# Rotary halves of queries and keys: exchanged by GpSimd's product with the sines in place of transfers

## Chip, cores and metric

The kernel runs on one core of a Trainium2 chip. The metric is the device time of one execution in microseconds (us). The parts of the core that appear below are PE (TensorE, the matmuls) and its weight loads (PEld), DVE (VectorE), ACT (ScalarE), POOL (GpSimd), SP (SyncE, here only a queue that issues transfers), and the 16 transfer engines. A transfer is issued by a queue (SP's, ACT's or POOL's own) and lands some microseconds later.

## What is computed

All data are float32. First comes an attention of one head of 256 over two batches of 1024 positions, with norms around it, and then a layer with 16 heads of 128 and a mixture of four experts. The change lies in the second layer's attention:

```python
q = (h @ wq + bq).reshape(b, s, H, HD).transpose(0, 2, 1, 3)
k = (h @ wk + bk).reshape(b, s, H, HD).transpose(0, 2, 1, 3)
...
def _rotate_half(x):
    x1, x2 = jnp.split(x, 2, axis=-1)
    return jnp.concatenate((-x2, x1), axis=-1)
...
q = q * cos + _rotate_half(q) * sin
k = k * cos + _rotate_half(k) * sin
scores = jnp.einsum('bhqd,bhkd->bhqk', q, k) / math.sqrt(HD)
scores = jnp.where(causal[None, None], scores, jnp.finfo(jnp.float32).min)
probs = jax.nn.softmax(scores.astype(jnp.float32), axis=-1).astype(q.dtype)
out = jnp.einsum('bhqk,bhkd->bhqd', probs, v)
```

Each of the 128 entries of a head's query or key is multiplied by a cosine, and the entry 64 places away is multiplied by a sine (negative for the first 64) and added.

## The kernel before

**Tiling.** A unit is one head of one batch: 8 rows of 128 queries against up to 1024 keys (the causal half). There are 32 units, two heads of the same weight columns form a pair, so 16 pairs. A query or key tile (`Twq`, `Twk`) has the 128 entries of a head along the 128 partitions and the 1024 positions along the free dimension. So the entry 64 places away lies in another partition, in the same column.

**Steps.** The order of the work is written out by hand: the whole kernel is a list of steps, one per row, and each step (`step`, L954) issues the scores of its row, then "fillers" that were put at this step, then work of earlier rows. One step in the steady part takes about 3.5 us. While PE goes through the 8 rows of a pair's first unit, the fillers compute the values of this pair and the keys of the next; in the second unit they compute the output product of the pair before and the queries of the next pair. Keys, queries and values of a pair are made by seven products in place of eight (`seven_products`, L539), which need sums of weight blocks that POOL computes (`weight_sums`, L522) and queries' weights scaled by POOL (`scale_queries`, L459).

**The rotation.** Whenever 512 columns of a query or key tile are written, by ACT (L502, L584) or DVE (L592), `rotated` (L465) is called. It issues two transfers on SP's queue at once: partitions 64 to 127 of the tile to partitions 0 to 63 of a tile `rot` (L469), and the other half (L470). `rot` has two buffers. It also appends `rest` to a list, and the step that follows, at its end, runs it: the tile times the cosines (L474), `rot` times the sines (L475), and their sum (L476), all 128 partitions by 512 columns, all on POOL. The argument `eng` of L474 is POOL's engine in every call, since `HELP` is empty. There are 128 rotations.

**The gathers.** The probabilities of a row are computed by DVE (L319, L321) and ACT (L326), scaled by ACT (L717) and transposed in blocks of 32 by DVE (L734) into one of two buffers (`pair_sb` for the first four rows of a unit, `x1`, shown as `x`, for the last four). Once four rows are there, `gather` (L745) issues 16 transfers on SP (L756), eight in each of two steps, that put the blocks into a tile `pT`. PE multiplies it with the values (L777). For the last four rows of a unit these products come 8 steps after the fourth row's scores, and 9 and 10 steps after them. So SP's queue, which issues strictly in its order, holds the exchanges of the rotation and the gathers, and the loads of the weights (L456) too.

**Other work on POOL.** The residual of the first layer (L436), the normalisation of `h` for the first batch (L204, in the last pair), and the issue of some loads. The cosines and sines are loaded once into `rope_sb` (L173).

Of the kernel before, what the change touches and what calls it, by code (L numbers as in the profile page):

```python
# [12 lines left out]
F32 = mybir.dt.float32  # L13
AF = mybir.ActivationFunctionType
ALU = mybir.AluOpType
# [3 lines left out]
P = 128  # L19
# [8 lines left out]
def kernel(  # L28
# [27 lines left out]
    nc = tc.nc  # L56
# [22 lines left out]
    bpool = ctx.enter_context(tc.tile_pool(name="bpool", bufs=2))  # L79
# [90 lines left out]
    bo_sb = const.tile([P, D], F32, name="bo_sb")  # L170
    nc.gpsimd.dma_start(bo_sb, bo.partition_broadcast(P))
    rope_sb = const.tile([P, 2, S], F32, name="rope_sb")
    nc.gpsimd.dma_start(rope_sb, rope.rearrange("k p s -> p k s"))  # L173

    par = const.tile([P, n_par], F32, name="par")

# [287 lines left out]

    def rotated(t, cs, eng=nc.gpsimd):  # L465

        rot = bpool.tile([P, 512], F32, tag="rot", name="rot")
        half = P // 2
        nc.sync.dma_start(rot[:half, :], t[half:, cs])  # L469
        nc.sync.dma_start(rot[half:, :], t[:half, cs])  # L470

        def rest():

            eng.tensor_tensor(t[:, cs], t[:, cs], rope_sb[:, 0, cs], ALU.mult)  # L474
            nc.gpsimd.tensor_tensor(rot, rot, rope_sb[:, 1, cs], ALU.mult)  # L475
            nc.gpsimd.tensor_tensor(t[:, cs], t[:, cs], rot, ALU.add)  # L476

        rope_later.append(rest)
# [9 lines left out]
    def b_project(u, name, n):  # L488

        g, b, hh = u  # L490
        bcol = cols["bq" if name == "wq" else "bk"] + g * GH + hh
        t = head_tile(u, name)
        pa = acc_tile()
        for c in range(DC):
            nc.tensor.matmul(
                pa,
                lhsT=wg[name][:, c, ts(hh, HD)],
                rhs=xT[:, c, ds(b * S + n * 512, 512)],
                start=(c == 0),
                stop=(c == DC - 1),  # L500
            )
        nc.scalar.activation(  # L502
            t[:, ts(n, 512)], pa, AF.Identity, bias=par[:, bcol : bcol + 1]
        )
        rotated(t, ts(n, 512))
# [33 lines left out]
    def seven_products(g, b, name, wide):  # L539
# [46 lines left out]
        def done(i, k):  # L586
            if not value:
                eng = nc.vector if (g, b) == pairs[1] and name in HELP else nc.gpsimd
                rotated(head_tile(heads[i - 1], name), ts(k - 1, 512), eng)
# [660 lines left out]
    s = A0 + (len(units) - 2) * NT  # L1250
# [154 lines left out]
```

## Time and profile before

| What | Value |
|---|---|
| time before, median of 3 runs | 1195.93 us (1195.11 to 1196.88) |
| the profiled execution, its own time | 1197.6 us |
| its span in the trace | 1195.8 us |
| instructions | 15503 |
| granted PE clock, mean | 0.996 |
| POOL's products of the rotation, L474 to L476 | 384, about 1.28 us each, 492.4 us |
| SP's issues: gathers / exchanges of halves | 976 / 256 |
| share of the 16 transfer engines taken by queue 1 | 51.4% |

The busy table gives each engine's busy time, its share of the span and the number of its instructions. A row of the groups of instructions has the line, engine, operation, output and inputs, the count, then busy time, mean duration of one in ns, and the idle time of the engine in front of them. Rows of transfer issues end with the median us from issue to landing. Rows of waits give who waited for whom, the total in us, the number of times and the longest one. A row of a queue in order of time gives its start, its length, engine, line and what it does, and in brackets the idle time before it. "x4" after a matmul counts records, of which a float32 matmul has two. A row of the table of stretches gives the stretch, its length, and the busy time of PE, PEld, DVE, ACT and POOL in it, then the PE clock, the share of the transfer engines, and GB/s. An engine that is named as the cause of a wait is inferred from semaphores, and can be another one that ended near by.

### The profile page before, as it was taken

To read this page: it belongs to the slowest core of one execution; us is meant where nothing else is said; L and a number is where in the kernel's file an instruction comes from. 1 tells how busy PE (TensorE), PEld (TensorE's weight loads), DVE (VectorE), ACT (ScalarE), POOL (GpSimd) and SP (SyncE) were. 2 spreads that over 40 slices of the span, in tenths; PEclk is the share of its full clock that TensorE was granted. 3 is DMA by queue.
4 is the path that set the end of the run, shared out by engine and by line. 5 is a ranking of instruction groups with operands and counts; after the bars stand their busy time and mean duration, and the time that the engine had idled before them with its cause. 6 is when DMAs were issued, how large, how long until landed. Compare 5 with 4: busy or idle time off the path is not lost.

```text
span 1195.8 us, 15503 instructions
## 1 busy us (share of the span) xinstructions
PE 1153.4 (96%) x4400; PEld 725.9 (61%) x4400; DVE 768.7 (64%) x1760; ACT 649.8 (54%) x1221; POOL 607.1 (51%) x594
## 2 busy tenths in 40 slices
PE   7999988989999999999999999999999999899997
PEld 5676644565656565656656565656565656556765
DVE  4554776656666766766676666666666567476565
ACT  3334356646565655656565656565656555453444
POOL 4005785566664747373837464666666667002100
PEclk9999999999999999999999999999999999999999
DMA  5001134777667667576666766666776767314011
GB/s 182 1 1 44 45 124 107 168 166 166 156 161 170 157 158 167 138 165 158 157 148 158 165 157 154 165 166 161 169 166 164 182 160 169 86 43 140 1 36 36
DMA packets 242391, 155.92 MB, mean 130 GB/s; under 512 B 21149, under 2 KB 223969, under 8 KB 241793
## 3 DMA queue, kind: packets, MB, share of 16 engines
q1 hardware_dynamic: 236720, 143.74, 51.4%
q0 software_dynamic: 2048, 5.94, 1.7%
q10 hardware_dynamic: 3536, 5.24, 1.2%
q8 instruction: 36, 0.59, 0.2%
q14 instruction: 51, 0.41, 0.1%
HBM read 20.62 MB, written 4.19 MB: 21 GB/s over the span
## 4 chain that ended last, share of the span: by engine, by line
PE 76%; SPq 7%; POOL 5%; DMA 5%; DVE 4%; issue 2%; ACT 1%; POOLq 0%; ACTq 0%; DVEq 0%
PE av L777 18%; PE sc L703 14%; PE pa L559 8%; PE pa L657 6%; SPq L756 6%; PE pa L550 5%; PE pa L1187 5%; PE pe L1210 4%; PE pc L559 3%; PE sc L360 3%; PE pa L382 2%; PE pc L550 2%; POOL rot L475 2%; DMA rot<-Twq 1%; POOL Twk L476 1%
## 5 line engine op out<-in xcount | busy, mean ns | idle before, releaser
L703 PE MATMUL sc<-Twk,Twq 128*128 128x512 f32 (+3 forms) x768 | 290.5, 487 | 2.2 <-ACT pr L326 1.3
L717 ACT ACTIVATE pr<-pr,rs 128x640 f32<-128x640 f32 (+1 forms) x244 | 190.0, 779 | 186.1 <-DVE rs L715 183.3
L777 PE MATMUL av<-pT,vg 128*128 128x512 f32 (+3 forms) x768 | 271.1, 491 | 19.2 <-DMA pT<-pair_sb 7.7
L326 ACT ACTIVATE pr<-sc,nmx 128x128 f32<-128x128 f32 (+7 forms) x272 | 201.0, 739 | 149.4 <-DVE nmx L321 122.8
L777 PEld LDWEIGHTS av<-pT,vg 128*128 128x128 f32 x768 | 142.4, 190 | 138.9 <-issue 101.5
L703 PEld LDWEIGHTS sc<-Twk,Twq 128*128 128x128 f32 x768 | 140.2, 191 | 125.3 <-issue 104.3
L321 DVE TENSOR_REDUCE nmx<-sc 128x1 f32<-128x128 f32 (+7 forms) x272 | 206.1, 758 | 9.4
L474 POOL TENSOR_TENSOR Twk<-Twk,rope_sb 128x512 f32<-128x512 f32 x64 | 82.0, 1280 | 201.2 <-DMA rot<-Twk 154.9
L319 DVE TENSOR_TENSOR sc<-sc,limit 128x128 f32<-128x128 f32 x272 | 79.6, 293 | 145.2 <-PE sc L703 129.8
L734 DVE STREAM_TRANSPOSE x<-pr 128x640 f32<-128x640 f32 (+1 forms) x124 | 128.8, 1039 | 60.8 <-DMA pT<-x 21.0
L475 POOL TENSOR_TENSOR rot<-rot,rope_sb 128x512 f32<-128x512 f32 x128 | 164.8, 1287 | 0.0
L657 PE MATMUL pa<-wo_g,aT 128*128 128x256 f32 x512 | 126.8, 381 | 0.0
L657 PEld LDWEIGHTS pa<-wo_g,aT 128*128 128x128 f32 x512 | 96.3, 191 | 35.2 <-issue 18.5
L474 POOL TENSOR_TENSOR Twq<-Twq,rope_sb 128x512 f32<-128x512 f32 x64 | 81.9, 1279 | 49.5 <-DMA rot<-Twq 33.1
L476 POOL TENSOR_TENSOR Twk<-Twk,rot 128x512 f32<-128x512 f32 x64 | 82.3, 1285 | 5.0
L476 POOL TENSOR_TENSOR Twq<-Twq,rot 128x512 f32<-128x512 f32 x64 | 81.4, 1271 | 5.0
L667 DVE TENSOR_TENSOR hx<-hx,pa 128x256 f32<-128x256 f32 (+1 forms) x124 | 52.4, 425 | 26.3 <-PE pa L657 24.0
L793 ACT ACTIVATE aT<-av,par 128x512 f32<-128x512 f32 x64 | 43.9, 686 | 42.8 <-PE av L777 42.7
L584 ACT ACTIVATE part<-pa,par 128x512 f32<-128x512 f32 x62 | 42.5, 687 | 39.7 <-PE pa L559 39.7
L734 DVE STREAM_TRANSPOSE pair_sb<-pr 128x128 f32<-128x128 f32 (+1 forms) x120 | 60.2, 502 | 2.8 <-DMA pT<-pair_sb 2.5
L1079 POOL TENSOR_TENSOR hx<-hx,x 128x256 f32<-128x256 f32 x16 | 12.7, 827 | 96.8 <-DVE hx L1219 84.6
L436 POOL TENSOR_TENSOR hx<-x,bo_sb 128x256 f32<-128x256 f32 x16 | 11.7, 733 | 90.7 <-ACT x L433 90.7
(193 smaller groups left out, 1620.7 us busy)
## 6 DMA issues: line engine op xcount, KB each, us to landing
pT<-x SPq DMA_DIRECT2D x496, 128.0 KB, 2.6
pT<-pair_sb SPq DMA_DIRECT2D x480, 64.0 KB, 2.1
rot<-Twk SPq DMA_DIRECT2D x128, 128.0 KB, 2.3
rot<-Twq SPq DMA_DIRECT2D x128, 128.0 KB, 2.3
wk_g<-in_L_ffn_wk_dram SPq DMA_DIRECT2D x9, 256.0 KB, 3.1
wq_g<-in_L_ffn_wq_dram SPq DMA_DIRECT2D x9, 256.0 KB, 3.2
wv_g<-in_L_ffn_wv_dram SPq DMA_DIRECT2D x9, 256.0 KB, 3.0
wo_g<-in_L_ffn_wo_dram SPq DMA_DIRECT2D x9, 256.0 KB, 3.0
```

The costliest lines, as they stand in the source:

```text
L321: nc.vector.tensor_reduce(nmx, sc[:, :L], AX.X, ALU.max, negate=True)
L326: nc.scalar.activation(pr[:, :L], sc[:, :L], AF.Exp, bias=nmx, accum_out=sm)
L474: eng.tensor_tensor(t[:, cs], t[:, cs], rope_sb[:, 0, cs], ALU.mult)
L475: nc.gpsimd.tensor_tensor(rot, rot, rope_sb[:, 1, cs], ALU.mult)
L476: nc.gpsimd.tensor_tensor(t[:, cs], t[:, cs], rot, ALU.add)
L550: nc.tensor.matmul(pa[:, ts(n, P)], lhsT=x[:, ts(n, P)], rhs=w, start=start and n == 0, stop=True, skip_group_check=True,)
L559: nc.tensor.matmul(pa, lhsT=w, rhs=x, start=start, stop=True, skip_group_check=True)
L657: nc.tensor.matmul(pa[:, ts(k, D)], lhsT=aT[g, b][:, hh, ts(i, P)], rhs=wg["wo"][:, hh, :], start=(hh == 0), stop=(hh == GH - 1),)
L703: nc.tensor.matmul(sc[:, ds(n0, n)], lhsT=qT[:, ts(i, P)], rhs=kT[:, ds(n0, n)], start=True, stop=True,)
L717: nc.scalar.activation(self.pr[:, :L], self.pr[:, :L], AF.Copy, scale=rs)
L734: nc.vector.transpose(z[:, i % 4, :n, :], self.pr[:, : n * 32].rearrange("p (m s) -> p m s", s=32))
L777: nc.tensor.matmul(cut(av), lhsT=vg[g, b][:, c, ts(hh, HD)], rhs=cut(pT[:, c, :]), start=(c == 0), stop=(c == i),)
```

## The change

`rotated` issues no transfers any more. Its deferred part takes the `rot` tile and lets POOL multiply partitions 64 to 127 of the tile by the sines, written to partitions 0 to 63 of `rot`, and then the other half the same way. The product with the cosines and the sum follow as before, on all 128 partitions. As the two inputs of such a product lie in the same partitions, the two halves of the sines are loaded exchanged, by two transfers in place of one for the whole table. On POOL, four instructions stand where three stood; the product with the cosines now comes after the ones with the sines, since it overwrites the tile that they read. On SP, the 256 exchanges are gone and nothing else is moved.

```diff
     rope_sb = const.tile([P, 2, S], F32, name="rope_sb")
-    nc.gpsimd.dma_start(rope_sb, rope.rearrange("k p s -> p k s"))
+    nc.gpsimd.dma_start(rope_sb[:, 0, :], rope[0])
+    for lo, hi in ((slice(0, P // 2), slice(P // 2, P)), (slice(P // 2, P), slice(0, P // 2))):
+        nc.gpsimd.dma_start(rope_sb[lo, 1, :], rope[1, hi])
...
     def rotated(t, cs, eng=nc.gpsimd):
 
-        rot = bpool.tile([P, 512], F32, tag="rot", name="rot")
-        half = P // 2
-        nc.sync.dma_start(rot[:half, :], t[half:, cs])
-        nc.sync.dma_start(rot[half:, :], t[:half, cs])
-
         def rest():
-
+            rot = bpool.tile([P, 512], F32, tag="rot", name="rot")
+            half = P // 2
+
+            for lo, hi in ((slice(0, half), slice(half, P)), (slice(half, P), slice(0, half))):
+                nc.gpsimd.tensor_tensor(rot[lo, :], t[hi, cs], rope_sb[hi, 1, cs], ALU.mult)
             eng.tensor_tensor(t[:, cs], t[:, cs], rope_sb[:, 0, cs], ALU.mult)
-            nc.gpsimd.tensor_tensor(rot, rot, rope_sb[:, 1, cs], ALU.mult)
             nc.gpsimd.tensor_tensor(t[:, cs], t[:, cs], rot, ALU.add)
 
         rope_later.append(rest)
```

## The prediction

> **What bounds the kernel now.** I read the busy table first, then the table of stretches, the waits of TensorE (PE), and last the queues in order of time around the longest wait.
>
> ```profile
> PE 1153.4 (96%) x4400; PEld 725.9 (61%) x4400; DVE 768.7 (64%) x1760; ACT 649.8 (54%) x1221; POOL 607.1 (51%) x594
> L475 POOL TENSOR_TENSOR rot<-rot,rope_sb 128x512 f32<-128x512 f32 x128 | 164.8, 1287 | 0.0
> rot<-Twk SPq DMA_DIRECT2D x128, 128.0 KB, 2.3
> rot<-Twq SPq DMA_DIRECT2D x128, 128.0 KB, 2.3
> 219.38:963.30 743.92, 734.99 (x2757) 450.64 (x2756) 486.38 (x1054) 443.05 (x833) 454.63 (x433) 1.00 0.69 162
> ```
>
> PE is busy for 96% of the span. The last line is the steady part, 26 units (one unit is one head of one batch): 734.99 of 743.92 us of PE, POOL (GpSimd) 454.63, clock 1.00. A unit takes 743.92/26 = 28.61 us, a pair of units 57.22. The quietest pair in the chain of waits (from the product at 609.09 to the one at 665.30) takes 56.21. So PE's own work is a floor: only what PE waits can be won, about 1.0 us a pair here, 13 us in all, and some at both ends.
>
> ```profile
> PE av L777 <- DMA pT<-pair_sb: 7.7, 3, 4.6
> PE av L777 <- DMA rot<-Twq: 6.7, 4, 3.6
> PE av L777 <- DMA pT<-x: 1.3, 1, 1.3
> ```
>
> These are PE's waits with their totals, counts and longest. All three are one kind: the product with the values (L777) waits for probabilities that L756's transfers bring. Eight of them, 15.7 us: 2.47 at 202.9, 3.58 at 249.0, 0.65 at 590.7, 0.69 at 817.8, 1.73 at 932.1, 1.34 at 990.6, 0.65 at 1003.7, 4.61 at 1020.7. Nothing else PE waits for is over 2.2 us between the loads at the start and the end. The SP queue ahead of the one at 249.0:
>
> ```profile
> 229.19 0.46 SPq L469 DMA_DIRECT2D rot<-Twq  x1
> 229.70 1.74 SPq L470 DMA_DIRECT2D rot<-Twq  x1
> 231.55 7.64 SPq L756 DMA_DIRECT2D pT<-x  x8
> 239.51 0.51 SPq L469 DMA_DIRECT2D rot<-Twq  x1
> 240.06 0.59 SPq L470 DMA_DIRECT2D rot<-Twq  x1
> 240.70 5.29 SPq L756 DMA_DIRECT2D pT<-x  x8
> ...
> 249.01 1.96 PE L777 MATMUL av<-pT,vg 128*128 128x512 f32 x3 [3.58 <-DMA rot<-Twq]
> ```
>
> SP issues without a gap, some 0.6 us a transfer, and the gathers stand in one line with the exchanges. The last gather is issued at 246.0, and lands 2.6 us later by the page's median: 248.6, just ahead of 249.0. A unit has 32 gathers (L756, 5.29/8 = 0.66 us each, 21.2 us) and 8 exchange issues (0.535 and 0.595 by their medians, 4.5 us): 25.7 of 28.6 us, before weight loads and waits. **SP's order of issue is the second bound behind PE.**
>
> **Part 1, the 256 exchanges leave SP.** This frees 4.5 us of issue a unit and the waits in which an exchange held the gathers: SP waited at L469 for POOL's addition (a free rot buffer) 19.8 + 8.9 us, for POOL's weight sums about 6.6, and early on for DVE's queries and keys 41.6. Twice 128 x 128 KB leave the transfer engines as well; I give that no price of its own.
> Per stall: at 249.0 four issues stood between 229.19 and 240.70, about 4 us with the 1.74, and the gathers in front of them were late by as much again; 3.58 goes. At 202.9 two issues (1.2 us) lie between the halves of the gather, and the one at 186.62 waited for DVE's sum in front of it: most of 2.47 goes. 590.7, 817.8 and 932.1 each have six or more issues within the last 14 us (over 3 us): 3.1 goes. 990.6, 1003.7, 1020.7: sixteen issues between 957.9 and 991.4, 9.1 us in a line with almost no gap till 1026; but weight loads on POOL's queue (issued 1011.7 to 1013.0) share the transfer engines, so I take 5.0 of 6.6. Sum 2.2 + 3.6 + 3.1 + 5.0 = 13.9.
> A product that starts after such a wait is recorded with 1.95 to 1.98 us for 1.72, and most pairs have one with a wait too short for the list. The 26 units hold 13 x 1.01 = 13.1 us above the quietest pair, 6.7 of it in the listed waits; of the other 6.4 I take half, 3.2. **Gain 17.1 us.**
> What is late next: the gather's own inputs, ACT's scaling (L717) and DVE's transposes (L734). Those waited for transfers themselves (26 us of DVE's L734 waits for gathers that still read its buffer), so they move forward with the gathers.
>
> **Part 2, POOL gets one product more per rotation.** Before, L474, L475, L476 start 1.23, 1.35 and 1.23 us apart: the third waits for POOL's own result and costs 0.12 more. 3.81 us. After: two products of 64 partitions, the product with the cosines (it overwrites what both read, so it waits), the sum (it waits). No row of the trace has a POOL product on 64 partitions, nor one that reads and writes different partitions.
> The nearest row is the 128 x 512 product: time there goes with the elements per partition (128x128 0.46, 128x256 0.73, 128x512 1.28 us), and a half has the same 512. So a half costs 1.23, and a rotation 1.23 + 1.35 + 1.35 + 1.23 = 5.16.
> The Trainium skill, "GPSIMD Engine Reference", section 2.1, says each of the eight cores serves its own 16 partitions and begins the next instruction once its share is done. If the core follows the written partition, the two halves use different cores and overlap: 3.9 us, almost no extra work. But the same page's split has a core reading and writing its own 16, and this product crosses over: that may cost extra, and the page has no price. I take the row, 5.16; ends 3.9 and 7.6 (each half twice the row).
> The page's section 4.1 speaks against the change: two-input elementwise work belongs on VectorE, GpSimd being about 2x slower. The rows agree on the ratio (POOL 1.28, DVE's L592 0.69), and by engine time the change loses: 128 x 1.35 = 173 us more on POOL. Read with the waits it doesn't: POOL idled 154.9 + 33.1 us before L474 for exchanges that are gone. By the rule +173 where POOL is the path, by the rows 0 where it isn't.
>
> ```profile
> POOL Twk L474 <- DMA rot<-Twk: 154.9, 28, 17.2
> POOL Twq L474 <- DMA rot<-Twq: 33.1, 18, 3.4
> 872.81 0.45 POOL L526 TENSOR_TENSOR S<-wv_g 128x128 f32<-128x128 f32 x1
> 876.63 0.38 PE L703 MATMUL sc<-Twk,Twq 128*128 128x128 f32 x2
> 880.78 1.05 PE L550 MATMUL pc<-S,lent 128*128 128x128 f32 x8
> ```
>
> The check is the fullest pair, where POOL also makes weight sums. Now its rotations start at 844.76, 850.72, 854.53, 859.50 (keys), 863.30, 869.01, eight sums from 872.81, then 876.62 and 880.43, done at 884.3. Afterwards, each free 2.4 us sooner: 842.4, 848.3, 853.5, 858.6, 863.8, 869.0, the first query done 869.0, the second 874.1, value sums done 876.0, key sums 877.9, end 888.2. PE reads the first query at 876.63 (7.6 us to spare), the value sums at 880.78 (4.8 to spare), the last queries a unit later. POOL's next work starts at 890. So it hides, with the 4.8 us as the cover: it is gone when twelve halves are 0.40 us dearer each, above 1.63.
> Other places: eight rotations from 101.7 to 138.1 end at about 146 instead; first readers are at 121.1 (keys and queries done 112) and 146.2 (done 123). Around 257.7 the query weights' load in POOL's queue goes 1.7 us later; its product is some 10 us off. The normalisation of h (L204, 1000.36 and 1006.90) stands behind the last rotation, which I put at 1001.3 for 999.7; PE transposes at 1009.7 and 1013.4, and comes some 2 us sooner relative to it: I charge 1.0.
>
> **Part 3, the sines** come as two loads and the cosines as one, in place of one: two more POOL issues of 0.74 us by 15 us, with POOL idle and the first rotation at 101.7. Nothing.
>
> **Sum.** Span 1195.8 - 17.1 + 1.0 = 1179.7; with 1.8 us around it the profiled execution would be 1181.5. That execution (1197.6) lies 1.7 above the median of the runs, 1195.93; median 1179.8, said as 1180.
>
> **Rivals.**
> A, likeliest: as above; 1173 to 1187, 0.66.
> B, the gathers are bound by their inputs, not by SP: freed issue time becomes SP idle time, and PE goes on waiting. For it: the eight gathers from 231.55 took 7.64 us, 2.4 more than 5.29, so some inputs were late. Against it: elsewhere SP runs gapless. A third to a half of the gain: 1187 to 1193, say 1190, 0.13.
> C, slower: the crossing makes each half dear. From 1.63 PE waits for value sums; from about 1.74 eight rotations and 7.1 us of sums and scaling no longer fit in 56.6 us, and POOL is the bound. At 2.46 a half a rotation takes 7.6, a pair 60.8 plus on average 4.9, 9.1 us too long; over some 14 pairs +127, less no gain: about 1320. For it: no row shows a crossing; against it: the flat dependence on elements. 0.14.
> D, it meets: halves near 1.6, gains and new stalls cancel; 1193.5 to 1198, 1196, 0.07. That the exchange goes on by transfers in another guise is excluded by the diff.
> If the halves overlap, A's time hardly moves, as POOL has cover already.
>
> A measurement of this kernel tells no change from one to about 0.2% (2.4 us). Faster: A and B, 0.79; same 0.07; slower 0.14. The range goes from A's low end, with 1 more for the unlisted waits, 1172, to 1195, which takes in B and part of D.
>
> **What would show it.** Right: no rot transfers on SP, gaps in SP's line between gathers, PE's waits at L777 under 5 us in all, POOL's halves at 1.23 to 1.28, POOL near 770 us busy, PE busy unchanged near 1153 to 1149. Wrong: halves at over 1.6 us, or PE waiting at L703 or L550 for POOL (C); L777 still waiting for pT with SP idle (B); a wait at the transposes of h near 1010 over 3 us.

## Result and profile after

| | before | after |
|---|---|---|
| median (4 runs each, beside one another) | 1195.52 us (1194.88 to 1196.88) | 1181.55 us (1179.69 to 1183.09) |
| ratio of the medians, 95% interval | | 0.9881 [0.9864, 0.9898] |
| the profiled execution | 1197.6 us, span 1195.8 | 1183.09 us, span 1181.3 |
| SP's exchanges of halves | 256 | 0 |
| queue 1, share of the transfer engines | 51.4% | 39.9% |

The change makes the kernel 1.2% faster; 1180.0 was predicted. The profiled execution is the slowest of the four after the change, so spans are compared with spans below.

The first view of the kernel after is the busy table with the groups of instructions and the queue's row (queue, packets, MB, share of the engines):

```profile
PE 1151.3 (97%) x4400; PEld 727.5 (62%) x4400; DVE 771.2 (65%) x1760; ACT 649.4 (55%) x1221; POOL 775.6 (66%) x724
L474 POOL TENSOR_TENSOR rot<-Twk,rope_sb 64x512 f32<-64x512 f32 x128 | 162.8, 1272 | 108.8 <-DVE Twk L592 102.2
q1 hardware_dynamic: 216240, 110.17, 39.9%
```

POOL has 168 us more to do and the kernel is faster. A product on 64 partitions takes 1.27 us, as one on 128 did (1.28). POOL now idles for the keys that DVE has yet to write, no longer for transfers.

Next, PE's waits in the kernel after (total, times, longest):

```profile
PE av L777 <- DMA pT<-pair_sb: 5.4, 2, 3.9
PE pt L340 <- DVE pr L719: 4.0, 2, 3.2
```

Of eight waits for gathers, 15.7 us, two are left, 5.4 us. The row of 3.2 us is new: before, that wait (at 149.73) was 1.44.

Last, the queue that changed. SP's largest wait between 280 and 900 us, after:

```profile
SPq L756 <- DVE rs L715: 131.0, 45, 5.1
```

and before:

```profile
SPq L469 <- POOL Twk L476: 12.3, 16, 1.1
```

SP waits 147.2 us in these 620 after, 31.1 before. Before, the gathers never waited long for the data they move: SP reached them late. After, SP stands at a gather until its blocks have been scaled and transposed (the cause named is DVE). The queue has turned from late to early.

**Where the time went.** The span is cut at the first score product of a unit; each stretch is the difference of two start times. The forecast's items are put into the stretch where their stalls lay.

| stretch | before | after | gain | forecast |
|---|---|---|---|---|
| A, start to unit 1 | 165.53 | 167.31 | -1.78 | 0 |
| B, units 1 and 2 (stall at 202.9) | 53.85 | 50.94 | 2.91 | 2.2 |
| C, units 3 and 4 (249.0) | 61.74 | 57.94 | 3.80 | 3.6 |
| D, units 5 to 26 (590.7, 817.8, short waits) | 623.27 | 618.11 | 5.16 | 1.3 + 3.2 |
| E, units 27 to 30 (932.1 to 1020.7, transposes of h) | 120.07 | 114.14 | 5.93 | 1.7 + 5.0 - 1.0 |
| F, unit 31 to the end | 171.34 | 172.86 | -1.52 | 0 |
| sum | 1195.8 | 1181.3 | 14.5 | 16.1 |

In D a pair takes 618.11/11 = 56.19 us, the floor of 56.21 that the quietest pair before had shown. The stretch from 280 to 900 us has PE busy throughout (columns as in the table of stretches before):

```profile
280.00:900.00 620.00, 620.00 (x2339) 382.24 (x2338) 414.25 (x894) 377.16 (x707) 496.69 (x447) 1.00 0.53 125
```

Beside 620.00 stands the count of 2339 matmul records. In the kernel before, the same stretch holds fewer:

```profile
280.00:900.00 620.00, 616.92 (x2325) 379.21 (x2325) 408.88 (x887) 373.31 (x701) 375.61 (x355) 1.00 0.69 160
```

**The loss in F.** PE idles as long in F as before (2.2 us); it is busy 1.54 us longer, at a lower granted clock:

```profile
1024.46:1195.80 171.34, 162.60 (x623) 109.59 (x622) 109.00 (x295) 75.36 (x120) 12.69 (x16) 0.99 0.19 53
1008.44:1181.30 172.86, 164.14 (x624) 110.30 (x622) 109.04 (x295) 75.43 (x121) 12.71 (x16) 0.98 0.19 53
```

In the kernel after, the clock stands at one half from 1017.89 to 1021.30; before, PE's work in F was at the full clock but for 0.3 us. So F's loss is time at half clock and no wait for POOL. Why the clock fell there is open: no wait of PE over 0.3 us stands ahead of it in F.

### The profile page after: what moved, and what is told of

Its sections match the earlier page's. It is cut to its first block, busy times and chain, and to the rows that moved or that the text cites. A ratio compares the mean times of both kernels' runs of the same rounds, so it can differ in the third digit from the quotient of the medians.

```text
span 1181.3 us, 15200 instructions
## 1 busy us (share of the span) xinstructions
PE 1151.3 (97%) x4400; PEld 727.5 (62%) x4400; DVE 771.2 (65%) x1760; ACT 649.4 (55%) x1221; POOL 775.6 (66%) x724
## 3 DMA queue, kind: packets, MB, share of 16 engines
q1 hardware_dynamic: 216240, 110.17, 39.9%
## 4 chain that ended last, share of the span: by engine, by line
PE 91%; DVE 4%; DMA 2%; SPq 1%; ACT 1%; issue 1%; ACTq 0%; DVEq 0%
PE av L777 21%; PE sc L703 19%; PE pa L559 10%; PE pa L657 9%; PE pa L550 5%; PE pa L1187 5%; PE pe L1210 4%; PE pc L559 4%; PE sc L362 3%; PE pa L384 2%; PE pc L550 2%; SPq L756 1%; PE pa L303 1%; PE pa L290 1%; DMA pT<-x 1%; PE pt L340 1%
## 5 line engine op out<-in xcount | busy, mean ns | idle before, releaser
L474 POOL TENSOR_TENSOR rot<-Twk,rope_sb 64x512 f32<-64x512 f32 x128 | 162.8, 1272 | 108.8 <-DVE Twk L592 102.2
L474 POOL TENSOR_TENSOR rot<-Twq,rope_sb 64x512 f32<-64x512 f32 x128 | 162.5, 1269 | 8.8
L734 DVE STREAM_TRANSPOSE x<-pr 128x640 f32<-128x640 f32 (+1 forms) x124 | 128.8, 1039 | 25.1 <-ACT pr L717 16.1
```

What stands on the lines that cost most here:

```text
L474: nc.gpsimd.tensor_tensor(rot[lo, :], t[hi, cs], rope_sb[hi, 1, cs], ALU.mult)
L734: nc.vector.transpose(z[:, i % 4, :n, :], self.pr[:, : n * 32].rearrange("p (m s) -> p m s", s=32))
```

## The cover on POOL, and what is left

The fullest pair of the kernel after, POOL in order of time:

```profile
862.65 0.46 POOL L529 TENSOR_TENSOR wv_g<-wv_g 128x128 f32<-128x128 f32 x1
...
865.08 2.59 POOL L474 TENSOR_TENSOR rot<-Twq,rope_sb 64x512 f32<-64x512 f32 x2
867.75 1.27 POOL L475 TENSOR_TENSOR Twq<-Twq,rope_sb 128x512 f32<-128x512 f32 x1
869.10 1.27 POOL L476 TENSOR_TENSOR Twq<-Twq,rot 128x512 f32<-128x512 f32 x1
```

and PE's reader of the value sums in the same trace:

```profile
870.70 1.05 PE L550 MATMUL pc<-S,lent 128*128 128x128 f32 x8
```

A rotation takes 5.4 us by these rows (forecast 5.16). The second half starts 2.59 - 1.27 = 1.32 us after the first, and in the trace it waits for no semaphore: the halves, on different partitions, do not overlap. The value sums end at 863.1 and are read at 870.70: 7.6 us to spare where 4.8 were forecast.

The larger remaining stall is the old one at 1020.7, now at 1004.80:

```profile
1004.80 3.37 PE L777 MATMUL av<-pT,vg 128*128 128x512 f32 x4 [3.91 <-DMA pT<-pair_sb]
```

In POOL's queue two loads of the last expert's weights and biases are issued just ahead of it:

```profile
997.35 0.78 POOL L1021 DMA_DIRECT2D lent<-in_L_ffn_we_dram  x1
998.13 0.59 POOL L1023 DMA_DIRECT2D lent<-in_L_ffn_be_dram  x1
```

The other one, 1.49 us at 245.78, stands behind the load of all experts (1 MB, issued at 226.0). Gathers that are issued beside such loads land late. From issue to landing (least, median, longest), over all gathers from 280 to 900 us, then for those issued from 997.5 to 1002.5 and from 226 to 229:

```profile
DMA to landing us min/median/max: 2.0/2.4/5.1
DMA to landing us min/median/max: 2.5/5.0/6.3
DMA to landing us min/median/max: 4.0/11.8/12.5
```

**The loss in A.** PE in the kernel after waits 3.20 us for the first layer's scaled probabilities:

```profile
150.98 0.87 PE L340 MATMUL pt<-ident,pr 128*128 128x128 f32 x3 [3.20 <-DVE pr L719]
```

DVE's chain to it, after:

```profile
146.95 0.93 DVE L417 SCALAR_TENSOR_TENSOR nb<-mva,rx 128x4 f32<-128x4 f32 x1
147.80 1.64 DVE L206 TENSOR_SCALAR pair_sb<-x,mva,rx 128x256 f32<-128x256 f32 x2
149.37 0.94 DVE L536 TENSOR_TENSOR xT<-xT 128x512 f32<-128x512 f32 x1
```

and before:

```profile
147.15 0.23 DVE L415 SCALAR_TENSOR_TENSOR nb<-mva,rx 128x4 f32<-128x4 f32 x1
147.30 1.16 DVE L204 TENSOR_SCALAR pair_sb<-x,mva,rx 128x256 f32<-128x256 f32 x2
148.38 0.68 DVE L536 TENSOR_TENSOR xT<-xT 128x512 f32<-128x512 f32 x1
```

The same instructions are 0.70 + 0.48 + 0.26 us longer, and L407 at 144.69 another 0.32 (0.49 for 0.17): 1.76 us, which is the whole growth of the wait from 1.44 to 3.20. What differs is POOL beside them. Before, it was idle from 138.9 to 146.6; after, the rotations of the start fill that time and push POOL's next work back:

```profile
146.60 1.26 POOL L476 TENSOR_TENSOR Twq<-Twq,rot 128x512 f32<-128x512 f32 x1
```

The tiny L417 ends at 147.88, when POOL's sum does (147.86), and L407 at 145.18, when a half product on POOL does (145.15). The Trainium skill, "SBUF — State Buffer", section "SBUF: two separate sides", says that DVE and GpSimd share a port pair as an exclusive lock, held for a whole instruction, against DVE instructions with two inputs in SBUF or in a two-port mode. These two ends agree; L407 has one input, and no row here shows an instruction's mode. L206 and L536 grow without such an end.

The growth of this wait equals A's loss of 1.78 us, but only by chance. Over all of A, PE idles just 0.3 us more (10.9 and 11.2), since other waits shrank. It is busy 1.4 us longer, as half the clock was granted after the longer wait, from 150.90 to 154.32:

```profile
0.00:165.53 165.53, 154.65 (x633) 105.28 (x634) 94.05 (x238) 62.97 (x136) 66.11 (x82) 1.00 0.21 60
0.00:167.31 167.31, 156.09 (x633) 106.32 (x634) 96.19 (x238) 62.91 (x136) 78.33 (x92) 0.99 0.14 44
150.98:153.98 3.00, 3.00 (x7) 1.88 (x8) 2.93 (x6) 1.75 (x4) 2.83 (x5) 0.50 0.42 175
```

The forecast asked when the first reader needs the rotations (9 and 23 us off) and not who works beside them.

## The experiments

The kernel before ran beside each of them; its median in these sessions was 1197.4 to 1197.8 us, so kernels are compared by their ratios to it. Question one is what made the gathers late: the time to issue the exchanges, the waits in which an exchange holds the queue, or the bytes. Question two is how far POOL's cover reaches and what its fourth product costs. Question three is what the last stalls are.

**Issue time alone** (`e2_small_back`): the kernel after, with two transfers of 8 columns per rotation put back on SP, that wait for no engine.

```diff
     def rotated(t, cs, eng=nc.gpsimd):
 
+        idle = bpool.tile([P, 8], F32, tag="idle", name="idle")
+        nc.sync.dma_start(idle[: P // 2, :], rope_sb[P // 2 :, 0, 0:8])
+        nc.sync.dma_start(idle[P // 2 :, :], rope_sb[: P // 2, 0, 0:8])
```

> The changed kernel, with two transfers put back on SP where each exchange was issued, but of 8 columns, from the table of cosines to a tile that nobody reads: only the time to issue comes back (about 4.5 us a unit), no bytes to speak of, and no wait for DVE, ACT or POOL. Theory 1a (issue time): 1188 to 1195 us. Theory 1b (what cost was SP standing in front of an exchange whose tile or buffer was not ready): 1180 to 1184 us.

Measured 1185.81 us, 0.9901 [0.9879, 0.9924]: between the two ranges expected, 0.2% above the kernel after, with overlapping intervals. Stretch D is 618.10, the floor. SP's largest wait for its gathers' inputs falls from 131.0 to this, in the same 620 us:

```profile
SPq L759 <- DVE rs L718: 8.6, 10, 2.0
```

So 256 issues do eat the time by which SP had become early, and that costs nothing in D, where something is left of it. That issue time is the price by which a stall is worked out, as the prediction did, is refuted for D. B is 52.14 for 50.94 and E 118.81 for 114.14; C is 56.69 for 57.94, as the stall at 245.78 is absent there.

**The exchange on another queue** (`e1_pool_queue`): the kernel before, with its exchanges issued by POOL's queue a step later, and the rest a step after that. All bytes move, SP has none of it.

```diff
-        nc.sync.dma_start(rot[:half, :], t[half:, cs])
-        nc.sync.dma_start(rot[half:, :], t[:half, cs])
+        def exchange():
+            rot = bpool.tile([P, 512], F32, tag="rot", name="rot")
+            half = P // 2
+            nc.gpsimd.dma_start(rot[:half, :], t[half:, cs])
+            nc.gpsimd.dma_start(rot[half:, :], t[:half, cs])
...
-        rope_later.append(rest)
+            rope_last.append(rest)
+
+        rope_later.append(exchange)
```

> The kernel before, but the exchange of the halves is issued by POOL's queue one step later, and the three products follow a further step later: all 256 transfers of 128 KB are still made, SP issues none of them, and POOL's work per rotation is 3.81 us plus two issues of 0.74, about as much as in the changed kernel. Theory 1 (the gain is SP's line of issue): 1178 to 1186 us, waits at L777 under 6 us. Theory 2 (the gain is that the exchanges' bytes no longer crowd the gathers): 1190 us or more, L777 still waiting some 15 us.

Measured 1256.45 us, 1.0485 [1.0452, 1.0517]; no theory had this. PE no longer waits for any gather. It waits for POOL:

```profile
PE sc L706 <- POOL Twq L477: 47.6, 12, 9.4
```

and POOL for its own exchanges to land:

```profile
POOL Twq L475 <- DMA rot<-Twq: 124.9, 52, 4.2
POOL Twk L475 <- DMA rot<-Twk: 110.4, 44, 5.5
```

So all the bytes, at a slower pace, do not make PE wait for gathers when SP is free of the exchanges, though the gathers themselves take longer to land (median 2.7 us for 2.4, from 280 to 900). And the wait for a transfer must not move onto the engine that works: here POOL stands still for 235 us.

**Full transfers into `rot`** (`e3_full_into_rot`): the kernel after, with both full transfers back, into the `rot` tile, though nothing needs their data.

```diff
+        rot = bpool.tile([P, 512], F32, tag="rot", name="rot")
+        half = P // 2
+        nc.sync.dma_start(rot[:half, :], rope_sb[half:, 0, cs])
+        nc.sync.dma_start(rot[half:, :], rope_sb[:half, 0, cs])
+
         def rest():
-            rot = bpool.tile([P, 512], F32, tag="rot", name="rot")
-            half = P // 2
```

> The changed kernel, with two transfers of 64 x 512 put back on SP where each exchange was issued, from the table of cosines into the rot tile, which POOL's products overwrite: issue time, bytes and SP's wait for a free rot buffer come back, not the wait for the tile of queries or keys. Theory 1a: within 3 us of the kernel with small transfers. Theory 1b: clearly more than that one, 1193 us or more. Theory 2: as 1b, with SP no later than there.

Measured 1248.91 us, 1.0423 [1.0403, 1.0443]: more than the kernel before, which moves the same bytes. SP's largest wait of that kernel:

```profile
SPq L471 <- POOL Twk L479: 180.6, 28, 87.9
```

Of these 180.6 us, 101.9 lie before 160 us or after 1100. PE's largest wait:

```profile
PE av L780 <- DMA pT<-x: 25.0, 9, 6.1
```

POOL's rotation is longer by one product, holds a `rot` buffer longer, and SP stands before it with gathers behind. One wait in an in-order queue is handed on to everything behind it.

**Large transfers without `rot`** (`f2_large_back`): as the first experiment, with 320 columns.

```diff
+        idle = bpool.tile([P, 320], F32, tag="idle", name="idle", bufs=1)
+        nc.sync.dma_start(idle[: P // 2, :], rope_sb[P // 2 :, 0, :320])
+        nc.sync.dma_start(idle[P // 2 :, :], rope_sb[: P // 2, 0, :320])
```

> The changed kernel with two transfers of 64 x 320 put back on SP where each exchange was issued, from the cosines to a tile that nobody reads: issue time and 5/8 of the old bytes, no wait for an engine. Theory 2 (bytes): some 5/8 of the loss above the small ones, 1190 or more. Theory 1b (waits): as with the small ones, 1183 to 1187.

Measured 1234.44 us, 1.0305 [1.0274, 1.0335]. It can't answer for bytes: with one buffer, SP waited for its own earlier transfer,

```profile
SPq L469 <- DMA idle<-rope_sb: 84.3, 63, 7.3
```

so it is a second showing of the experiment above, with transfers as the holder in place of POOL.

**All waits and issues, few bytes, and then all bytes** (`f1_small_all_waits`, `f3_full_all_waits`): a pair that differs in bytes alone. POOL has three products as before; the transfers go from the tile into `rot`, on SP, with the waits of the kernel before, with 8 columns in one and 512 in the other. The product with the sines reads the tile itself, so the exchange has no part in the output.

```diff
+        rot = bpool.tile([P, 512], F32, tag="rot", name="rot")
+        half = P // 2
+        few = slice(cs.start, cs.start + 8)
+        nc.sync.dma_start(rot[:half, :8], t[half:, few])
+        nc.sync.dma_start(rot[half:, :8], t[:half, few])
         def rest():
+            nc.gpsimd.tensor_tensor(rot, t[:, cs], rope_sb[:, 1, cs], ALU.mult)
...
-            for lo, hi in ((slice(0, half), slice(half, P)), (slice(half, P), slice(0, half))):
-                nc.gpsimd.tensor_tensor(rot[lo, :], t[hi, cs], rope_sb[hi, 1, cs], ALU.mult)
```

> The kernel with one product per rotation (exchange left out, 1178 us), with two transfers of 8 columns put back on SP in the old place, from the tile of queries or keys into the rot tile: all the old waits (SP for the tile and for a free rot buffer, POOL for the landing) and the issue time are back, of the bytes almost nothing. Theory 1 (issue and waits in SP's line): most of the loss is back, 1190 to 1197. Theory 2 (bytes): 1180 to 1185, near the changed kernel with small transfers.

> As the one with small transfers and all waits, but 64 x 512 each: everything that the exchange cost SP, POOL and the transfer engines is back, with three products on POOL, of which the sines now come first. Control: 1193 to 1199, like the kernel before. What lies between this and the small one is the bytes' share.

Measured 1191.86 us, 0.9951 [0.9938, 0.9964], with few bytes, as theory 1 had it, and 1201.18 us, 1.0031 [1.002, 1.0042], with all, a little over the range expected. PE's waits at the values' product say where, first with few bytes:

```profile
201.41 2.39 PE L779 MATMUL av<-pT,vg 128*128 128x512 f32 x8 [1.76 <-DMA pT<-pair_sb]
247.63 2.43 PE L779 MATMUL av<-pT,vg 128*128 128x512 f32 x4 [3.73 <-DMA rot<-Twq]
940.76 3.51 PE L779 MATMUL av<-pT,vg 128*128 128x512 f32 x8 [1.95 <-issue]
1015.06 3.75 PE L779 MATMUL av<-pT,vg 128*128 128x512 f32 x4 [5.83 <-DMA pT<-pair_sb]
```

Apart from one for DVE at 171.48, these are all over 0.4 us, and none lies between 250 and 940. With all bytes there are such rows there:

```profile
589.85 1.95 PE L779 MATMUL av<-pT,vg 128*128 128x512 f32 x4 [0.49 <-DMA rot<-Twq]
703.74 1.95 PE L779 MATMUL av<-pT,vg 128*128 128x512 f32 x4 [1.04 <-DMA pT<-x]
818.26 1.95 PE L779 MATMUL av<-pT,vg 128*128 128x512 f32 x4 [0.86 <-DMA pT<-x]
```

**One product of 128 partitions** (`e6_one_product`): no transfers, the exchange left out, three products on POOL.

```diff
-            for lo, hi in ((slice(0, half), slice(half, P)), (slice(half, P), slice(0, half))):
-                nc.gpsimd.tensor_tensor(rot[lo, :], t[hi, cs], rope_sb[hi, 1, cs], ALU.mult)
+            nc.gpsimd.tensor_tensor(rot, t[:, cs], rope_sb[:, 1, cs], ALU.mult)
```

> The changed kernel with one 128-partition product in place of the two halves (the exchange of halves is left out): POOL does three products per rotation, as before, and SP no exchanges. If POOL's extra product is hidden except at the start: the time of the changed kernel less about 2 us (PE's wait at 151 goes back from 3.2 to 1.4), 1177 to 1181. If it costs something all along: 1176 or less.

Measured 1178.19 us, 0.9846 [0.9829, 0.9864]. With the two kernels above, the one before and the one after, by stretch, cut as above:

| stretch | before | no exchange | few bytes, all waits | all bytes, all waits | after |
|---|---|---|---|---|---|
| A | 165.53 | 163.95 | 164.52 | 164.44 | 167.31 |
| B | 53.85 | 51.31 | 53.34 | 53.78 | 50.94 |
| C | 61.74 | 56.22 | 61.91 | 62.96 | 57.94 |
| D | 623.27 | 618.10 | 618.47 | 624.20 | 618.11 |
| E | 120.07 | 114.83 | 121.21 | 119.08 | 114.14 |
| F | 171.34 | 171.79 | 171.65 | 172.84 | 172.86 |

This table answers question one by place, for D clearly, for the rest in part. In D, eleven of the sixteen pairs, the issues and waits cost 0.4 us without the bytes and 6.1 with them: the bytes decide there, through a landing of 2.3 us for 1.7 to 1.8, and through `rot` being held longer (SP's waits from 280 to 900 grow from 29.5 to 37.1 us). Which of these two counts for more stays open. The gathers' own landing is not it: its median is 2.4 us in both kernels, from 280 to 900. In B, C and E, ahead of the steady part and behind it, the issues and waits cost 2.0 + 5.7 + 6.4 = 14.1 us with hardly a byte moved. In C issues alone took 56.69, so it takes the waits; in B and E issues alone gave 52.14 and 118.81. But C and E are also where the experts' loads land from POOL's queue. Before, the gather issued at 231.55 lands 7.9 us later, behind the 1 MB load issued at 229.9. No run has the exchange without these loads, so how much of C and E the waits would cost alone is not known.

**Halves to the same partitions** (`e5_same_side`): the kernel after, without the crossing.

```diff
-                nc.gpsimd.tensor_tensor(rot[lo, :], t[hi, cs], rope_sb[hi, 1, cs], ALU.mult)
+                nc.gpsimd.tensor_tensor(rot[hi, :], t[hi, cs], rope_sb[hi, 1, cs], ALU.mult)
```

> The changed kernel, but each half product is written to the partitions it reads, so the halves are not exchanged (the rotation itself is left out, everything else is the same). If crossing to the other 64 partitions costs nothing, a half stays at 1.27 us and the second starts 1.33 us after the first. If crossing costs something, the same-side half is shorter, or the two halves overlap.

One run, 1182.74 us. The halves of that kernel:

```profile
L474 POOL TENSOR_TENSOR rot<-Twk,rope_sb 64x512 f32<-64x512 f32 x128 | 163.0, 1273 | 107.8 <-DVE Twk L592 101.2
```

1273 ns for 1272: writing to other partitions costs this product nothing. The forecast's unknown with the wide ends (up to 2.46 us a half) is settled at its nearest row.

**More work on POOL** (`e7_plus_128`, `e8_plus_512`): a fifth product per rotation, whose result is not used, of 128 or of 512 columns.

```diff
         def rest():
...
+            spare = bpool.tile([P, 128], F32, tag="spare", name="spare")
+            nc.gpsimd.tensor_tensor(spare, rope_sb[:, 0, :128], rope_sb[:, 1, :128], ALU.mult)
```

> The changed kernel with one more product of 128 x 128 per rotation on POOL, 0.54 us: a rotation 5.9 us. By the cover of 7.6 us, of which six rotations take 3.2: no change within 2 us, 1179 to 1184. If the cover was already used up: 1186 or more.

> The changed kernel with one more product of 128 x 512 per rotation on POOL (overwritten by the halves), 1.34 us: a rotation 6.7 us instead of 5.38. If POOL's work hides behind a cover of 7.6 us (the changed kernel's value sums end at 863.1, PE reads them at 870.7): six rotations take 8.0 of it, and four pairs in a row with sums need 60.9 us of 56.2, so PE begins to wait for POOL at L703 or L550: 1188 to 1206 us. If POOL has cover without limit: 1180 to 1184.

With 0.54 us more a rotation: 1179.92 us, 0.9859 [0.984, 0.9878], not told apart from the kernel after, and D is 618.10. Two effects cancel in this, though. B is 52.60 for 50.94, with a first wait of PE for a rotation,

```profile
193.97 0.46 PE L705 MATMUL sc<-Twk,Twq 128*128 128x128 f32 x2 [0.80 <-POOL Twq L478]
```

and E is 109.73 for 114.14, as the stall at 1004.80 is absent (more on this below). With 1.34 us more: 1230.22 us, 1.0272 [1.0254, 1.0291], well over what was expected. Its busy table and PE's waits:

```profile
PE 1166.2 (95%) x4400; PEld 733.3 (60%) x4400; DVE 774.7 (63%) x1760; ACT 652.4 (53%) x1221; POOL 933.2 (76%) x852
```

```profile
PE sc L704 <- POOL Twq L477: 12.9, 7, 3.9
PE pc L551 <- POOL S L527: 10.4, 8, 2.6
```

The place is that of the rival "crossing makes a half dear": PE waits for queries and weight sums from POOL. Its price was too low. By its sum, eight rotations of 6.6 us and 4.9 of other work are 57.7 us a pair, 1.1 over the 56.6 then taken, some 16 us in all; the kernel is 49 us slower than after. D alone gives 635.71 - 618.11 = 17.6; the rest lies in A, B, C and E (A is 176.40). And PE's own busy time is 15 us longer, at a mean granted clock of 0.980 for 0.994. Such a bound must be summed by stretch. POOL's cover thus ends between 0.54 and 1.34 us a rotation in D; in B the first wait shows at 0.54.

A also answers the loss at the start: 163.95 to 165.53 in the four kernels of the table with three products, 166.7 to 168.6 in all those with four, 176.40 with the largest fifth. In the kernel without the exchange the wait at L340 is back at 1.4 us and the clock after it at 1.00. That POOL's work there causes the loss is shown; that it acts through the shared port is read from the rows, and no run took the port alone away.

**Loads out of the gathers' way** (`e9_loads_later`, `e10_loads_later_both`): the kernel after, with the last expert's loads issued a step later on SP, behind the gathers; the second also issues the load of all experts six units later.

```diff
-    at(A0 + 30 * NT + 6, load_second, (3,))
+    at(A0 + 30 * NT + 7, load_second, (3,), nc.sync)
...
-    at(A0 + 3 * NT, load_experts)
+    at(A0 + 9 * NT, load_experts)
```

> The changed kernel, with the last expert's weights (256 KB) and the experts' biases (512 KB) loaded from SP behind the gathers of that step, not from POOL's queue at 997 to 999 us. If these loads hold up the gather that PE waits 3.9 us for at 1000.9: that wait goes below 1 us, and the time is 3 to 6 us below the changed kernel's, 1175 to 1178. If the gather is late by itself: the wait stays, 1180 to 1183.

> The kernel with the last loads behind the gathers (1177.8 us), and the first experts' weights (1 MB) loaded 6 units later, in the steady part. If that load holds up the gather that PE waits 1.5 to 1.9 us for near 245: the wait goes, 1174 to 1177. If SP's slack in the steady part doesn't cover it: a new wait at L777 near 395, no gain.

Measured 1177.77 us, 0.9836 [0.9811, 0.9861], and 1175.75 us, 0.9822 [0.9794, 0.985]. In the first the stall of 3.91 us is this:

```profile
1002.59 1.96 PE L777 MATMUL av<-pT,vg 128*128 128x512 f32 x4 [0.54 <-DMA pT<-pair_sb]
```

In the second, C is 56.22 for 57.94 and E 110.13 for 114.14; all that PE still waits for a gather is

```profile
PE av L777 <- DMA pT<-pair_sb: 0.3, 1, 0.3
```

Both last stalls were loads on POOL's queue, landing while gathers did. It is the moment that counts, not the queue: in the kernel after, two gathers of that product's `x` are issued behind the first of the last loads, at 997.61 and 998.27, and land more than 6 us later; in the kernel with 0.54 us more on POOL the same load is issued from POOL's queue at 999.70, behind the last such gather (999.37), and PE doesn't wait. The second of the two kernels is the fastest that was run: 1.8% under the kernel before, its interval wholly below that of the kernel after.

## Why the prediction was right, and where not

The likeliest case, A, came: 1180.0 said, 1181.55 measured, a span shorter by 14.5 us for the 16.1 worked out.

- **The floor and what can be won.** Right to 0.02 us a pair.
- **The stalls.** Six of eight are gone; PE's waits for gathers are 5.4 us, where under 5 was named as a sign. B, C and D gained 1.6 us more than their items: 0.7 of it in B, 0.2 in C, and 0.7 in D, which fell to its floor, with all of its short waits and not half.
- **The reason for it.** This step was right in its object, SP's line, and wrong in its term. It priced a stall by the issue time standing in front of it, and gave the bytes no price. The runs show issue time alone, added to the kernel after, to cost nothing in D, 1.2 us in B and 4.7 in E; waits and issues act ahead of D and behind it, and in D almost nothing happens without the bytes, whose share there is 624.20 - 618.47 = 5.7 us. Its showcase, the stall at 249.0, it read as SP's order alone; the gathers there also landed late behind the experts' load, which it didn't look at. That the sum came out is in part luck: the exchange took all three away together.
- **The last three stalls.** "I take 5.0 of 6.6" was too much at 1020.7: of 4.61 us only 0.70 went, and 2.7 of the 6.6 in all. With the 1.73 at 932.1 this makes 4.4; the other 1.5 of E's 5.93 came from waits too short for the list and from products that follow no wait any more. The prediction named the loads on POOL's queue as the reason for caution; they were the cause, as the run with later loads shows.
- **POOL.** The row was the right price (1.32 us from start to start for the 1.23 taken, 5.4 a rotation for 5.16), and the overlap that the page on GpSimd allowed did not come. The sums were covered with more room than worked out, as rotations started still earlier.
- **The start.** Priced at nothing, it lost 1.78 us. The missing steps are POOL's slowing of DVE beside it, and the half clock that followed PE's longer wait.
- **The normalisation of h.** The 1.0 us charged did not come: POOL was done with its last rotation at 986.2, and no transpose waits for it. F lost 1.52 us for another reason, time at half clock, which has no term in the prediction. Over all kernels F varies from 171.2 to 173.2 us.
- **The rivals.** B's sign showed (SP does wait for its gathers' inputs), but PE does not wait with it. C's mechanism exists, and its threshold was not reached.

## What to carry to other kernels

A transfer in an in-order queue has three prices, its issue time, its wait with everything behind it, and the time of its bytes; look at whether the queue is early (it waits for its inputs) or late (it never does) before charging the first, for an early queue gives it for nothing. Work can move to an engine that idles half of its time, at a dearer price per element, if the sum is made for the fullest stretch and not over the kernel, and if the engines beside it are asked too. When a stall stays though its supposed cause is gone, look for what lands at the same time from another queue.

## What was not expected of the hardware

**A stall costs more than its length.** The granted clock just after three waits (stretch, length, busy times, then the clock), before, after the wait of 4.61 us:

```profile
1020.70:1024.50 3.80, 3.79 (x9) 1.88 (x10) 3.23 (x6) 2.83 (x5) 0.00 (x0) 0.59 0.38 90
```

and after the change, behind those of 3.91 and 1.49 us:

```profile
1004.80:1008.00 3.20, 3.20 (x4) 1.36 (x5) 3.17 (x6) 2.25 (x3) 0.00 (x0) 0.55 0.44 103
245.78:248.00 2.22, 2.22 (x6) 1.21 (x7) 2.19 (x4) 0.93 (x1) 2.16 (x2) 1.00 0.43 101
```

The four records of the product take 3.10 and 3.37 us at the low clock, 1.96 at the full one, so such a stall costs another 1.1 to 1.4 us. The wait of 3.58 at 249.0 was followed by 0.66. After the waits of 3.58, 3.91 and 4.61 us the clock stood at one half for 3.41 us each.

How long must a wait be for this? In the traces of all fourteen kernels, PE waits 136 times for 1 us or more, counted from 100 us on and where the wait began at the full clock. After none of the 74 waits up to 1.87 us the clock fell, and after all 41 of 3.17 us and more it did. Of the 21 between, 11 lost it and 10 did not. Two of these, behind the wait of 2.47 us at 202.94 before, and behind 1.95 us at 940.76 with few bytes:

```profile
202.94:205.94 3.00, 3.00 (x15) 2.21 (x16) 1.64 (x6) 1.85 (x4) 0.00 (x0) 1.00 0.85 192
940.76:943.76 3.00, 3.00 (x7) 1.78 (x8) 1.47 (x6) 1.28 (x3) 0.44 (x1) 0.69 1.20 227
```

The Trainium skill, "TensorE: Matmul & The Clock Gate", section "HAM oscillation — how this bites in real kernels", asks for no idle gap of PE above about 3.4 us. Here that is too long: the wait of 3.20 us in A of the kernel after was followed by 0.50. What decides between 1.9 and 3.1 us stays open.

**A product on half the partitions takes the full time**, 1.27 us, and two such products on different partitions run one after the other, 1.32 us apart.
